# Gate rows, waiting outputs and the fill of a sorted buffer in a two-layer mixture of experts

## The chip, the cores and the metric

The kernel runs on one core of a Trainium2 chip, in float32. The metric is the device time in microseconds of one execution; the time shown is the median of several runs. A profile is one more execution, taken by the hardware profiler, with its own (longer) time.

A core has a matrix engine (TensorE, PE in the profile; PEld are its weight loads), a vector engine (VectorE, DVE), an activation engine (ScalarE, ACT), GpSimd (POOL) and SyncE (SP), which here only issues DMAs. Each engine runs its own list of instructions in order and waits on semaphores. Matrix products land in PSUM and are read from there by DVE or ACT.

## The reference, cut to what matters

Two layers work on `x` of 8 x 256 tokens of 128 numbers (16 tiles of 128 tokens). Each has a conditioning part and a mixture of 8 experts with a hidden width of 512. In the first layer every expert is computed for every token, and weighted with a gate; in the second only the two best experts of a token are.

```python
# first layer: x + ffn0(pool(x))
logits = jnp.einsum('bld,ed->ble', x, gate_weight)
kth_val = jnp.sort(logits.reshape(-1))[expert_k - 1]
gates = logits * (logits >= kth_val)
h = gelu(jnp.einsum('bld,ehd->bleh', x, w1) + b1, approximate=True)
y = jnp.einsum('bleh,edh->blde', h, w2) + b2.T[None, None]
out = jnp.einsum('blde,ble->bld', y, gates)
...
# second layer: x + ffn1(adapt(x)), with xn = layernorm(x) * gamma + beta
w, idx = jax.lax.top_k(softmax(xn @ gate_w), 2)
w = w / jnp.sum(w, axis=-1, keepdims=True)
h = gelu(jnp.einsum('bld,edh->eblh', xn, w1) + b1, approximate=False)
output = sum over experts of cw * (h @ w2 + b2) + residual
```

What matters here: the gates of the first layer need the k-th smallest of all 16384 logits, so no gate is known before all tokens have been pooled and the threshold has been found; the experts' outputs themselves don't need it.

## The kernel before, in words

**Units.** The 16 token tiles are worked in five units (`UNITS`): three of four tiles (512 columns), two of two tiles (256 columns). In `layer`, for each unit and each expert, four matmuls `hp` (w1 times the pooled tokens, 128x512 each) go to PSUM and through ACT (GELU) to `hT`; four matmuls `yp` (w2 times `hT`) accumulate in one PSUM tile of the pool `psy`, which has two buffers. Each float32 matmul shows as two passes in the trace.

**The pump.** After every `hp` and every `yp` matmul, eight times per expert, `layer` calls `pump()`. It takes one step of the coroutine at the head of `behind`, so that the small chains are spread between the matmuls in program order: first the rest of the pooling, then `threshold()` (a search for the gate limit), then `adapt(u)` for each unit whose first layer is complete. `adapt` has the second layer's front end: residual (`x2T`, `fp`), the language adapter (`adp`, `ha`, `dp`), two layer norms, the top two experts, and for each token two scatters of its row into `xs`.

**Gates.** At its end, `threshold()` sends the gate table (`gate`, transposed to `gT`) to DRAM on POOL's queue (`gd_L<-gT_L`, L415) and puts it in the dict `gd0`. From there `accumulate(u, e, ...)` loads one row of it for one unit and expert, broadcast to all 128 partitions (`gbc`, 256 KB, on SP's queue, four buffers), and VectorE multiplies the expert's output with it and sums.

**Waiting outputs.** As long as there is no gate table, ACT copies an expert's output from PSUM to SBUF (`y_first`, L782) and a closure is appended to `waiting`. When the table is there, every second pump takes one from `waiting`. A later output goes straight from PSUM to VectorE (L753) once `waiting` is empty. `accumulate` writes the accumulator at expert 0 and adds to it for the others (L755), and at expert 7 it appends `adapt(u)` to `behind`. `adapt(0)` begins with `GATES_GAP` = 20 empty steps.

The scheduler that builds the program keeps the data dependences and a priority by program order, but may put a ready instruction of an engine ahead of one that it expects to wait; the order on each engine is fixed when the program is built.

**The sorted rows.** The second layer works on `xs`, a DRAM buffer of 8 x 2048 + 128 rows of 130 numbers (520 bytes: a token, its destination row, its weight), one region per expert. It is filled beforehand with zeros and with a destination that no output has (`NOWHERE`), by one DMA on SP's queue from a tile `empty` of one row per partition (L526); before it on SP stand the weights' loads, behind it the gate rows. Tokens are then scattered into it, and 39 tiles of 128 rows are fetched, each with its expert's weights (`fetch`, `turn`, `hidden`, `output`), and scattered to `ys` by POOL. A last step gathers `ys` and adds the residual.

Of the kernel before, what the change touches and what calls it, by code (L numbers as in the profile page):

```python
# [10 lines left out]
F32 = mybir.dt.float32  # L11
I32 = mybir.dt.int32
AF = mybir.ActivationFunctionType
# [7 lines left out]
B, S, D = 8, 256, 128  # L21
P = 128
NT = B * S // P
NG = 4
GT = NT // NG
GN = GT * P

UNITS = [(0, 0, 4), (1, 0, 4), (2, 0, 4), (3, 0, 2), (3, 2, 2)]
NU = len(UNITS)
SLOTS = {2: 17, 3: 21, 4: 39}  # L30
E, HC = 8, 4
# [7 lines left out]
ROWS = E * RCAP  # L39
RW = D + 2  # L40
# [3 lines left out]
SEARCH = 16  # L44
SEARCH_GAP = 3
CHAIN_GAP = 5
GATES_GAP = 20
LEAD = 6


# [3 lines left out]
C_B10 = C_G1 + E  # L54
C_B20 = C_B10 + E * HC
# [9 lines left out]
def tile_adaln_ffn_d2(ctx: ExitStack, tc: tile.TileContext, x, ptype, lang, cols, b1v,  # L65
                      w10, w20, w11d, w21d, lw1, lw2, lgb, out):
    nc = tc.nc
# [3 lines left out]
    const = ctx.enter_context(tc.tile_pool(name="const", bufs=1))  # L71
    first = ctx.enter_context(tc.tile_pool(name="first", bufs=E))
    keep = ctx.enter_context(tc.tile_pool(name="keep", bufs=NG))
    work = ctx.enter_context(tc.tile_pool(name="work", bufs=2))
    small = ctx.enter_context(tc.tile_pool(name="small", bufs=4))
    dram = ctx.enter_context(tc.tile_pool(name="dram", bufs=1, space=DRAM))
# [23 lines left out]
    w10s, w20s = [], []  # L100
    for e in range(E):
        t = first.tile([P, WW], F32, tag="w1", name=f"w10_{e}")
        nc.sync.dma_start(out=t[:, :HC * P], in_=w10[e])
        w10s.append(t)
        t = const.tile([P, HC, D], F32, name=f"w20_{e}")
# [49 lines left out]
    for b in range(B):  # L155
        at = nc.values_load(lgi[0:1, b:b + 1], engines=(SP,), min_val=0, max_val=NL - 1,
                            skip_runtime_bounds_check_because="a language's number")
        for lst, name, src, rows, width in (
# [3 lines left out]
            t = const.tile([rows, width], F32, name=f"{name}_{b}")  # L162
# [9 lines left out]
    xT, poolT, resid, gd0 = {}, {}, {}, {}  # L172
    done = set()

    def scratch(name):
        return work.tile([P, 2, S], F32, tag="scr", name=name, bufs=NSCR)
# [82 lines left out]
    fwd, bwd, rows = fwd[:B, :], bwd[:B, :], top[:B, :]  # L259
# [88 lines left out]
    def poolings():  # L348
# [33 lines left out]
    begun = const.tile([P, NT], F32, name="begun")  # L382
# [7 lines left out]
    kth = const.tile([P, NSLOT], F32, name="kth")  # L390
    nc.gpsimd.iota(kth, pattern=[[1, NSLOT]], base=0, channel_multiplier=0,
                   allow_small_or_imprecise_dtypes=True)
    empty = const.tile([P, RW], F32, name="empty")
    nc.gpsimd.memset(empty, 0.0)

    steps = const.tile([P, SEARCH + 1, 3], I32, name="steps")
    nc.gpsimd.memset(steps, 0)
    for k, low in enumerate((*range(29, 0, -2), 0)):
        nc.gpsimd.tensor_scalar(steps[:, k, :], kth[:, 1:4], float(1 << low), None, ALU.mult)
    nowhere = const.tile([P, 1], F32, name="nowhere")  # L400
    nc.gpsimd.memset(nowhere, float(NOWHERE))

    b2p = pss.tile([E, P], F32, tag="sm", name="b2p")
# [87 lines left out]
    def top_one(v, name):  # L491
# [13 lines left out]

    xs = dram.tile([ROWS + P, RW], F32, name="xs")
    ys = dram.tile([2 * NT * P, D], F32, name="ys")
    last, lists, scatters = [None], {}, []  # L510
    used = const.tile([P, E], F32, name="used")
# [3 lines left out]
    w21 = const.tile([P, E, HC * D], F32, name="w21")  # L515


    nc.gpsimd.tensor_copy(empty.bitcast(I32)[:, D:D + 1], nowhere)
    nc.sync.dma_start(out=w11x[:, :, :HC * P], in_=w11d)
    nc.sync.dma_start(  # L520
        out=w11x[:, :, HC * P:HC * P + HC].rearrange("e p c -> p e c"),
        in_=col[:, C_B11:C_B11 + E * HC].rearrange("p (e c) -> p e c", e=E))
    nc.sync.dma_start(out=w11x[:, :, HC * P + HC:], in_=b2r.unsqueeze(1).to_broadcast([E, P, D]))
    for e in range(E):
        nc.sync.dma_start(out=w21[:, e, :], in_=w21d[e].rearrange("p c d -> p (c d)"))
    nc.sync.dma_start(out=xs.rearrange("(m p) c -> p m c", p=P),  # L526
                      in_=empty.unsqueeze(1).to_broadcast([P, (ROWS + P) // P, RW]))

    def cumulated(f, name):
        c3 = small.tile([P, E, E], F32, tag="c3", name=f"c3_{name}", bufs=2)  # L530
# [5 lines left out]
    def tiles_of(counts, edges, name):  # L536

        c2 = small.tile([P, E, NT], F32, tag="c2", name=f"c2_{name}", bufs=2)
        nc.vector.tensor_tensor(c2, counts.unsqueeze(2).to_broadcast([P, E, NT]),
                                edges.unsqueeze(1).to_broadcast([P, E, NT]), ALU.is_ge)  # L540
        f = small.tile([P, E], F32, tag="f", name=f"nf_{name}")
        nc.vector.tensor_reduce(f, c2, AX.X, ALU.add)
        return f
# [32 lines left out]
    def adapt(u, acc):  # L576
        g, o, nt = UNITS[u]
        n, t0 = nt * P, g * GT + o
        batches = range(t0 // 2, (t0 + nt) // 2)
        for _ in range(GATES_GAP if u == 0 else 0):  # L580
            yield
        x2T = work.tile([P, GN], F32, tag="x2T", name=f"x2T{u}")[:, :n]
        nc.vector.tensor_tensor(x2T, acc, xT[g][:, o * P:o * P + n], ALU.add)
        yield
# [28 lines left out]
        zr = [work.tile([P, GT, RW], F32, tag="zr", name=f"zr{u}_{s}", bufs=4)[:, :nt, :] for s in range(2)]  # L613
# [67 lines left out]
        for s, oh in enumerate((oh1, oh2)):  # L681
# [5 lines left out]
            for t in range(nt):  # L687
                move = nc.gpsimd.indirect_dma_start(  # L688
                    out=xs, out_offset=bass.IndirectOffsetOnAxis(ap=pos[:, t:t + 1], axis=0),
                    in_=zr[s][:, t, :], in_offset=None)  # L690
# [8 lines left out]
        if u in SLOTS:  # L699

            k0, k1 = SLOTS.get(u - 1, 0), SLOTS[u]
            f = tiles_of(counts, begun if u == NU - 1 else full, str(u))
# [15 lines left out]
    waiting = deque()  # L718

    def run(key, steps):  # L720
        yield from steps
        done.add(key)

    pumps = itertools.count()

    def pump():
        if waiting and gd0 and next(pumps) % 2:
            waiting.popleft()()
        if behind:
            if next(behind[0], done) is done:  # L730
                behind.popleft()

    def finished(key):
        while key not in done:
            pump()

    def layer(name, act, sources, w1s, w2s, cb1, cb2, gates, before, then):


        accs = {}  # L740

        def accumulate(u, e, y, bias):
            g, o, nt = UNITS[u]
            n, t0 = nt * P, e * NT + g * GT + o
            gbc = work.tile([P, GN], F32, tag="gbc", name=f"gbc_{name}{u}_{e}", bufs=4)[:, :n]
            nc.sync.dma_start(out=gbc, in_=gates[0][t0:t0 + nt, :].rearrange("t p -> (t p)").partition_broadcast(P))  # L746
            if e == 0:
                accs[u] = work.tile([P, GN], F32, tag="acc", name=f"acc_{name}{u}", bufs=3)[:, :n]
            part = accs[u] if e == 0 else work.tile([P, GN], F32, tag="part", name=f"part_{name}{u}_{e}")[:, :n]
            if bias is None:  # L750
                nc.vector.tensor_tensor(part, y, gbc, ALU.mult)  # L751
            else:
                nc.vector.scalar_tensor_tensor(part, y, bias, gbc, ALU.add, ALU.mult)  # L753
            if e:
                nc.vector.tensor_tensor(accs[u], accs[u], part, ALU.add)  # L755
            if e == E - 1:
                behind.append(run((name, u), then(u, accs[u])))

        for u, (g, o, nt) in enumerate(UNITS):
            n = nt * P  # L760
            finished((before, g))
            for e in range(E):
                hT = work.tile([P, HC, GN], F32, tag="hT", name=f"hT_{name}{u}_{e}")[:, :, :n]
                for c in range(HC):
                    hp = psb.tile([P, GN], F32, tag="big", name=f"hp_{name}{u}_{e}_{c}")[:, :n]
                    nc.tensor.matmul(hp, lhsT=w1s[e][:, c * P:(c + 1) * P], rhs=sources[g][:, o * P:o * P + n],  # L766
                                     start=True, stop=True)
                    nc.scalar.activation(hT[:, c, :], hp, act,  # L768
                                         bias=col[:, cb1 + e * HC + c:cb1 + e * HC + c + 1])
                    if nt == GT or c % 2:  # L770
                        pump()
                yp = psy.tile([P, GN], F32, tag="y", name=f"yp_{name}{u}_{e}")[:, :n]
                for c in range(HC):
                    nc.tensor.matmul(yp, lhsT=w2s[e][:, c, :], rhs=hT[:, c, :], start=(c == 0), stop=(c == HC - 1))  # L774
                    if nt == GT or c % 2:
                        pump()
                b2 = col[:, cb2 + e:cb2 + e + 1]
                if gates and not waiting:
                    accumulate(u, e, yp, b2)
                else:  # L780
                    y = scratch(f"y_{name}{u}_{e}").rearrange("p a b -> p (a b)")[:, :n]
                    nc.scalar.activation(y, yp, AF.Identity, bias=b2)  # L782
                    waiting.append(lambda u=u, e=e, y=y: accumulate(u, e, y, None))

    behind.append(run("poolings", poolings()))
    behind.append(run("threshold", threshold()))
    layer("first", AF.Gelu_apprx_tanh, poolT, w10s, w20s, C_B10, C_B20, gd0, "pool", adapt)


    def listing(k):  # L790
# [132 lines left out]
```

## Time and profile before

| | us |
|---|---|
| median of 3 runs (389.3 to 390.95) | 389.63 |
| the profiled execution | 397.35 |
| its span, first to last instruction | 395.6 |
| the 28 products with fresh outputs, L753 (128x512: 0.75 each) | 17.2 |
| the 8 products with waiting outputs, L751 (0.69 each) | 5.5 |
| the 8 copies of waiting outputs, L782 (0.69 each) | 5.5 |
| the fill `xs<-empty`, first to last packet | 57 to 108 |

The profile's page gives busy times by engine, then the span in 40 slices of 9.9 us with a digit for each engine's busy share in tenths and for the clock that TensorE was granted. A table of waits has: engine, what waited, `<-` what it waited for, then total us, times, longest us. The chain of waits is followed back from the last instruction and has start, us, what. The timeline has start, us, engine, line, operation, names, shapes, and in brackets the idle time before it and what ended it. Busy time by stretch has the stretch, its length, and for PE, PEld, DVE, ACT and POOL busy us and the number of instructions, then the granted clock, the DMA share and GB/s.

The stages, from the timeline: loading, scores and pooling until about 45 us; the threshold search beside unit 0's experts until 87 us; the first layer until 293 us; the second layer's 39 tiles until 381 us; the last gather until 395.6 us.

### The profile page before, as it was taken

To read this page: it belongs to the slowest core of one execution; us is meant where nothing else is said; L and a number is where in the kernel's file an instruction comes from. 1 tells how busy PE (TensorE), PEld (TensorE's weight loads), DVE (VectorE), ACT (ScalarE), POOL (GpSimd) and SP (SyncE) were. 2 spreads that over 40 slices of the span, in tenths; PEclk is the share of its full clock that TensorE was granted. 3 is DMA by queue.
4 is the path that set the end of the run, shared out by engine and by line. 5 is a ranking of instruction groups with operands and counts; after the bars stand their busy time and mean duration, and the time that the engine had idled before them with its cause. 6 is when DMAs were issued, how large, how long until landed. Compare 5 with 4: busy or idle time off the path is not lost.

```text
span 395.6 us, 5983 instructions
## 1 busy us (share of the span) xinstructions
PE 358.8 (91%) x1657; PEld 241.8 (61%) x1657; DVE 192.4 (49%) x773; ACT 172.9 (44%) x396; POOL 100.8 (25%) x161
## 2 busy tenths in 40 slices
PE   7899999999965999999999999998999869999930
PEld 7596444444422445444544578866878869999930
DVE  6368665530066666355621356665845553333305
ACT  2046345446250232424243434424454646888830
POOL 8400000000000130712070012072215553555430
PEclk9999999999996999999999999999999997999985
DMA  6935789999997211312031001125634666888417
GB/s 186 370 73 171 149 255 190 151 226 146 148 157 171 58 34 28 86 21 53 28 81 26 16 25 40 38 66 125 189 103 140 179 180 178 225 227 233 120 40 287
DMA packets 49800, 51.63 MB, mean 131 GB/s; under 512 B 6580, under 2 KB 35518, under 8 KB 49768
## 3 DMA queue, kind: packets, MB, share of 16 engines
q1 hardware_dynamic: 45128, 44.79, 50.8%
q0 software_dynamic: 2400, 4.37, 3.3%
q10 hardware_dynamic: 2240, 2.10, 1.5%
q8 instruction: 14, 0.23, 0.3%
q14 instruction: 18, 0.15, 0.1%
HBM read 36.77 MB, written 17.02 MB: 136 GB/s over the span
## 4 chain that ended last, share of the span: by engine, by line
PE 59%; POOL 9%; DMA 9%; issue 8%; DVE 8%; SPq 3%; ACT 2%; POOLq 1%; DVEq 0%; ACTq 0%
PE yp_first L774 23%; PE hp_first L766 19%; POOL ys L843 7%; DMA gbc_first<-gd_L 4%; DMA gd_L<-gT_L 3%; PE hps L824 2%; PE yps L837 2%; PE poolp L294 1%; DMA yg<-ys 1%; PE top L272 1%; PE idle L207 1%; PE dp L600 1%; PE adp L593 1%; SPq L746 1%; PE atp L212 1%
## 5 line engine op out<-in xcount | busy, mean ns | idle before, releaser
L768 ACT ACTIVATE hT_first<-hp_first,col 128x512 f32<-128x512 f32 (+1 forms) x160 | 93.0, 602 | 119.8 <-PE hp_first L766 109.7
L774 PE MATMUL yp_first<-hT_first,w 128*128 128x512 f32 (+1 forms) x320 | 124.0, 521 | 10.4 <-DVE acc_first L753 7.5
L766 PE MATMUL hp_first<-poolT,w 128*128 128x512 f32 (+1 forms) x320 | 120.7, 512 | 0.1
L774 PEld LDWEIGHTS yp_first<-hT_first,w 128*128 128x128 f32 x320 | 59.0, 193 | 55.0 <-issue 37.5
L766 PEld LDWEIGHTS hp_first<-poolT,w 128*128 128x128 f32 x320 | 59.0, 190 | 43.1 <-issue 38.4
L827 ACT ACTIVATE hs<-hps,wt 128x128 f32<-128x128 f32 x156 | 44.5, 371 | 15.0 <-PE hps L824 10.3
L843 POOL DMA_INDIRECT ys<-yt,xt x39 | 38.5, 987 | 46.9 <-ACT yt L842 34.7
L824 PE MATMUL hps<-xc,wt 128*128 128x128 f32 x312 | 43.4, 283 | 5.5 <-issue 3.2
L688 POOL DMA_INDIRECT xs<-zr,pos x32 | 31.4, 980 | 63.6 <-DVE pos L686 28.8
L824 PEld LDWEIGHTS hps<-xc,wt 128*128 128x128 f32 x312 | 39.8, 199 | 6.5 <-issue 3.4
L837 PE MATMUL yps<-w,hs 128*128 x312 | 42.1, 279 | 0.6 <-ACT hs L827 0.6
L753 DVE SCALAR_TENSOR_TENSOR part_first<-yp_first,col,gbc_first 128x512 f32<-128x512 f32 (+1 forms) x28 | 17.2, 614 | 45.8 <-PE yp_first L774 42.7
L837 PEld LDWEIGHTS yps<-w,hs 128*128 128x128 f32 x312 | 38.8, 195 | 0.9 <-ACT hs L827 0.9
L841 DVE TENSOR_TENSOR yt<-yps,wt 128x128 f32<-128x128 f32 x39 | 11.4, 291 | 45.3 <-PE yps L837 37.3
L591 POOL MEMSET ha<- 1x512 f32 x5 | 2.6, 517 | 76.2 <-PE dp L600 76.1
L842 ACT ACTIVATE yt<-yt,xt 128x128 f32<-128x128 f32 x39 | 15.8, 405 | 13.5 <-DVE yt L841 6.5
L755 DVE TENSOR_TENSOR acc_first<-acc_first,part_first 128x512 f32<-128x512 f32 (+1 forms) x35 | 20.3, 580 | 0.6
L415 POOL DMA_DIRECT2D gd_L<-gT_L x1 | 0.7, 664 | 72.7 <-DVE gT_L L413 72.7
L782 ACT ACTIVATE y_first<-yp_first,col 128x512 f32<-128x512 f32 x8 | 5.5, 687 | 27.5 <-PE yp_first L774 27.5
L817 DVE TENSOR_SCALAR xc<-xtp,col 128x128 f32<-128x128 f32 x39 | 15.7, 403 | 1.2 <-PE kp L672 0.6
L429 DVE TENSOR_SCALAR_CACHE_REDUCE fl<-logit,tr 128x128 f32<-128x128 f32 x46 | 13.6, 344 | 0.6
L751 DVE TENSOR_TENSOR acc_first<-y_first,gbc_first 128x512 f32<-128x512 f32 x1 | 0.7, 693 | 23.0 <-DMA gbc_first<-gd_L 23.0
(207 smaller groups left out, 317.5 us busy)
## 6 DMA issues: line engine op xcount, KB each, us to landing
wt<-w11x SPq DMA_DIRECT2D x39, 322.0 KB
xs<-empty SPq DMA_DIRECT2D x1, 8385.0 KB
w<-in_w_dram SPq DMA_DIRECT2D x24, 256.0 KB
gbc_first<-gd_L SPq DMA_DIRECT2D x24, 256.0 KB
xt<-xs SPq DMA_DIRECT2D x39, 65.0 KB
w11x<-in_w_dram SPq DMA_DIRECT2D x1, 2048.0 KB
gbc_first<-gd_L SPq DMA_DIRECT2D x16, 128.0 KB
lgb<-in_lgb_dram SPq DMA_DIRECT2D x8, 128.0 KB
```

Source lines behind the costliest of these rows:

```text
L688: move = nc.gpsimd.indirect_dma_start(out=xs, out_offset=bass.IndirectOffsetOnAxis(ap=pos[:, t:t + 1], axis=0), in_=zr[s][:, t, :], in_off ...
L753: nc.vector.scalar_tensor_tensor(part, y, bias, gbc, ALU.add, ALU.mult)
L755: nc.vector.tensor_tensor(accs[u], accs[u], part, ALU.add)
L766: nc.tensor.matmul(hp, lhsT=w1s[e][:, c * P:(c + 1) * P], rhs=sources[g][:, o * P:o * P + n], start=True, stop=True)
L768: nc.scalar.activation(hT[:, c, :], hp, act, bias=col[:, cb1 + e * HC + c:cb1 + e * HC + c + 1])
L774: nc.tensor.matmul(yp, lhsT=w2s[e][:, c, :], rhs=hT[:, c, :], start=(c == 0), stop=(c == HC - 1))
L817: nc.vector.tensor_scalar(xc, tp, col[:, C_LG:C_LG + 1], col[:, C_LB:C_LB + 1], ALU.mult, ALU.add)
L824: nc.tensor.matmul(hp[:, c, :], lhsT=wt[:, c * P:(c + 1) * P], rhs=xc, start=True, stop=True)
L827: nc.scalar.activation(hT[:, c, :], hp[:, c, :], AF.Gelu, bias=wt[:, HC * P + c:HC * P + c + 1])
L837: nc.tensor.matmul(yp, lhsT=hT[:, c, :], rhs=w21[:, bass.ds(ek, 1), c * D:(c + 1) * D], start=(c == 0), stop=(c == HC - 1))
L842: nc.scalar.activation(yt, yt, AF.Copy, scale=xt[:, D + 1:D + 2])
L843: move = nc.gpsimd.indirect_dma_start(out=ys, out_offset=bass.IndirectOffsetOnAxis(ap=xt.bitcast(I32)[:, D:D + 1], axis=0), in_=yt, in_off ...
```

## The change

Four things are changed:

- The fill of `xs` is written in pieces of four rows: `empty` has four rows per partition (and takes one of the four buffers of the tag `zr`), `xs` is 512 rows longer than the regions instead of 128, and each partition fills a contiguous stretch of it, in 4224 pieces of 2080 bytes instead of 16512 of 520.
- `pump` counts from the moment the gate table is in `gd0`. After `GATES_GAP` = 16 pumps it hands the table to `layer` (by the new list `gates0`) and begins with the waiting outputs: one at every fourth pump (`DRAIN`), two per expert. `adapt(0)` has no empty steps at its head any more.
- From that moment on every new output goes straight from PSUM to VectorE, also while others are waiting.
- `accumulate` takes a unit's experts in any order: the first to come begins the accumulator, a counter `missing` tells the last.

```diff
-GATES_GAP = 20
+GATES_GAP = 16
+DRAIN = 4
...
-    empty = const.tile([P, RW], F32, name="empty")
+    empty = work.tile([P, GT, RW], F32, tag="zr", name="empty", bufs=4)
...
-    nowhere = const.tile([P, 1], F32, name="nowhere")
+    nowhere = const.tile([P, GT], F32, name="nowhere")
...
-    xs = dram.tile([ROWS + P, RW], F32, name="xs")
+    xs = dram.tile([ROWS + GT * P, RW], F32, name="xs")
...
-    nc.gpsimd.tensor_copy(empty.bitcast(I32)[:, D:D + 1], nowhere)
+    nc.gpsimd.tensor_copy(empty.bitcast(I32)[:, :, D], nowhere)
...
-    nc.sync.dma_start(out=xs.rearrange("(m p) c -> p m c", p=P),
-                      in_=empty.unsqueeze(1).to_broadcast([P, (ROWS + P) // P, RW]))
+    rows = xs.rearrange("(p m t) c -> p m (t c)", p=P, t=GT)
+    nc.sync.dma_start(out=rows, in_=empty.rearrange("p t c -> p (t c)").unsqueeze(1).to_broadcast(list(rows.shape)))
...
-        for _ in range(GATES_GAP if u == 0 else 0):
-            yield
...
-    pumps = itertools.count()
+    ready = itertools.count(-GATES_GAP)
+    gates0 = []
 
     def pump():
-        if waiting and gd0 and next(pumps) % 2:
-            waiting.popleft()()
+        if gd0:
+            n = next(ready)
+            if not n:
+                gates0.append(gd0[0])
+            if waiting and n >= 0 and n % DRAIN == 0:
+                waiting.popleft()()
...
-        accs = {}
+        accs, missing = {}, [E] * NU
...
-            if e == 0:
+            begun = u in accs
+            if not begun:
                 accs[u] = work.tile([P, GN], F32, tag="acc", name=f"acc_{name}{u}", bufs=3)[:, :n]
-            part = accs[u] if e == 0 else work.tile([P, GN], F32, tag="part", name=f"part_{name}{u}_{e}")[:, :n]
+            part = work.tile([P, GN], F32, tag="part", name=f"part_{name}{u}_{e}")[:, :n] if begun else accs[u]
...
-            if e:
+            if begun:
                 nc.vector.tensor_tensor(accs[u], accs[u], part, ALU.add)
-            if e == E - 1:
+            missing[u] -= 1
+            if not missing[u]:
                 behind.append(run((name, u), then(u, accs[u])))
...
-                if gates and not waiting:
+                if gates:
                     accumulate(u, e, yp, b2)
...
-    layer("first", AF.Gelu_apprx_tanh, poolT, w10s, w20s, C_B10, C_B20, gd0, "pool", adapt)
+    layer("first", AF.Gelu_apprx_tanh, poolT, w10s, w20s, C_B10, C_B20, gates0, "pool", adapt)
```

## The prediction

> **What bounds the kernel now.** I read the page first (busy shares and slices), then the table of waits, then the chain of waits and the timeline from 80 to 130 us, then busy time by stretch, and last the packets of the DMA queues.
>
> ```profile
> span 395.6 us, 5983 instructions
> PE 358.8 (91%) x1657; PEld 241.8 (61%) x1657; DVE 192.4 (49%) x773; ACT 172.9 (44%) x396; POOL 100.8 (25%) x161
> PE   7899999999965999999999999998999869999930
> PEclk9999999999996999999999999999999997999985
> DMA  6935789999997211312031001125634666888417
> ```
>
> TensorE is the bound: a slice is 9.9 us, and PE stands at 8 or 9 from slice 1 to the tail, but for slices 11 and 12 (109 to 128 us) and slice 32 (317 to 326). In slice 12 the clock digit falls to 6. DMA is full in slices 6 to 11. That is one place, and the table of waits names it:
>
> ```profile
> DVE acc_first L751 <- DMA gbc_first<-gd_L: 23.0, 1, 23.0
> PEld yp_first L774 <- DVE acc_first L753: 8.3, 1, 8.3
> PE yp_first L774 <- DVE acc_first L753: 7.5, 1, 7.5
> ```
>
> VectorE stood 23.0 us for the first gate row; PE then stood 7.5 us for VectorE to read an output out of PSUM. The chain of waits shows how the row came late, and the timeline the end of the stall:
>
> ```profile
> 87.83 11.58 DMA gd_L<-gT_L
> 99.42 2.84 SPq L746
> 103.54 11.18 DMA gbc_first<-gd_L
> 115.56 5.32 DMA gbc_first<-gd_L
> ```
> ```profile
> 110.57 0.69 DVE L751 TENSOR_TENSOR acc_first<-y_first,gbc_first 128x512 f32<-128x512 f32 x1 [23.04 <-DMA gbc_first<-gd_L]
> 121.00 0.69 DVE L751 TENSOR_TENSOR part_first<-y_first,gbc_first 128x512 f32<-128x512 f32 x1 [0.42 <-DMA gbc_first<-gd_L]
> 122.22 0.74 DVE L753 SCALAR_TENSOR_TENSOR acc_first<-yp_first,col,gbc_first 128x512 f32<-128x512 f32 x1
> 123.02 5.84 PE L774 MATMUL yp_first<-hT_first,w 128*128 128x512 f32 x8 [7.49 <-DVE acc_first L753]
> ```
> ```profile
> 116.00:123.00 7.00, 0.00 (x0) 0.00 (x0) 6.01 (x11) 0.25 (x1) 0.00 (x0) 0.82 0.91 192
> 123.00:128.00 5.00, 4.99 (x7) 2.21 (x8) 2.42 (x4) 0.00 (x0) 0.00 (x0) 0.56 0.75 134
> ```
>
> The gate table leaves at 87.8 us and lands 11.6 us later; the first row (a 256 KB broadcast load) needs another 11. Only then do the eight waiting outputs of unit 0 go through VectorE, one after the other, from 110.6 to 122.2, and behind them stands the one instruction that PE needs: the multiply that frees the PSUM buffer of unit 1, expert 0 (L753 at 122.2). There are two such buffers, so PE stops at expert 2. Its first eight passes afterwards take 5.84 us where eight take 3.43 elsewhere in the chain: 2.4 us lost to a clock of 0.56. So this place costs 7.5 + 2.4 = 9.9 us.
>
> What fills the DMA is `xs<-empty`, 8385 KB in 520-byte packets. They run from 57 to 108 us by the packet records, on the same queue that the gate rows use; their rate changes between some 272 GB/s (57 to 62 us, 80 to 83) and some 150 (63 to 77, 88 to 107).
>
> **What the Trainium skill says.** "DMA: Bandwidth & Descriptors", section "Queues, rings and completion order": each engine consumes a queue's descriptors in ring order and goes round between queues packet by packet. The trace agrees: the gate rows, on the fill's queue, start moving in earnest only as its last packets go (packets of 2048 B from 103 us), while the table, on POOL's queue, gets through in between, late. Same page, "Why small descriptors are slow (HBM only)": a fixed 3 cycles per packet beside 32-byte beats; an estimate from it is 20 cycles for 520 B and 68 for 2080, so 15% fewer per byte. "TensorE: Matmul & The Clock Gate", part 1: the clock halves after an idle window of about 3.4 us; the trace's 7.5 us of idle with 0.56 behind it agrees. "Runtime: NRT & Kernel Launch", on the launch: a profile's total exceeds the reported time by some 6.2 us whatever the kernel.
>
> **The change part by part.** The order of instructions on each engine shows that it moves things only between 87 us and the end of unit 2; from there on it is the same to the last instruction.
>
> *1. Order of the sums.* VectorE now gets, after the first waiting output, the multiply of unit 1 expert 0, then waiting outputs and fresh ones mixed: 12 gate rows (8 of unit 0, 4 of unit 1) ahead of unit 0's final sum, where there were 8. The same 8 outputs are held back and copied by ACT. Cost in instructions: none. Effect: the multiply that frees PSUM is second in the queue instead of after eight outputs. With the loads as late as now, it would run at 111.3 to 112 us (the second row was there at 111.2) instead of 122.2. PE wants the buffer at 115.5 in the order of before, and at 118.8 in the new one, since the scheduler puts expert 4's four `hp` matmuls (eight passes, 3.43 us) ahead too. The 9.9 us go.
>
> *2. The fill.* 4224 packets of 2080 B for 16512 of 520, 2% more bytes. Nothing in the trace shows 2080-byte stores of this kind; nearest are the 2048-byte packets before it, at 300 to 375 GB/s. Bounds: no faster than now in its slow stretches (150 GB/s, end at 109), or 350 throughout (end at 82). I take 15% off: an end near 100, gate rows a few us earlier. Below nothing: 2% more bytes, 1 us. It issues nothing more on SP; POOL's memset grows from 130 to 520 columns, under 1 us before 20 us, while the fill is issued at 53.5.
>
> *3. The pause.* GATES_GAP moves from unit 0's adaptation to the pumps behind the gates: 16 pumps are two experts, so the first row is summed at the end of unit 1 expert 0. Unit 0's adaptation now begins one expert later in PE's order; its chain to the scatters keeps its spacing (16 layer matmuls from `dp` to `znp`, 4 from `l1p` to `kp`). Later units start at the same places, so nothing behind is late.
>
> *4. What is late next.* With PE unbroken from 88 us, expert 2's outputs run at 118.8 to 122.2, 3's to 125.7, 4's to 129.1, then bare on PE stand `fp`, `adp`, `dp` of unit 0. `fp` wants unit 0's sum. Its last row's load reuses the buffer that expert 2's multiply frees at 123.1; a load in the quiet stretch took 1.0 us from the freed buffer to its first packet and 2.0 to the last (130.6 to 132.7), so it lands at about 126.5. Behind it: product, two sums and x2T at 0.61 us each, done at 129.4. `fp` (0.6) is unhindered, `adp` (1.0) ends at 130.7, and `dp` waits for two 0.47 us `ha` behind `x2`: PE idle some 0.7 us. With the old row spacing (one in about 1.75 us from 110.5) the twelfth is there at 129.8 and PE loses 2.7 us instead. I take 1.0.
>
> Sum: 9.9 - 1.0 = 8.9 us off, 395.6 to 386.7 in span. The profiled execution took 397.35, of which 1.75 lie around the span; the median of the runs is 389.63, 7.7 below. The skill's 6.2 us would explain most of that as overhead, so I carry the 8.9 over whole: 380.7, and write 381.0. Everything behind it is PE-bound or hangs on PE's order (the second layer with its 39 tiles, the wait near 322 us, the tail from 381), and moves along.
>
> **The rivals.**
>
> *A, the forecast (0.80):* the stall goes, 381.0. Its own range is 378.8 (no new wait, and the 0.4 and 0.3 us that PE idles at 147 and 156 gone too) to 386.
>
> *B (0.11): the stall is mostly the profile's.* The DMA shows two speeds; had the fill run at 272 GB/s all along, it would have ended at 57.5 + 31.6 = 89 us, the table would land at about 91.5, a row at 94.5, fifteen operations of 0.61 later PSUM is free at 104, and PE never stops. Unprofiled runs, 7.7 us shorter, could look like that. Then the change brings nothing and adds its 1.0: 390.6. Against it: PE runs at full clock in the profile, and other waits must share the 7.7. A half-size stall gives some 385, within A.
>
> *C (0.09), slower: PE runs into `fp` behind the twelfth row.* In PE's fixed order nothing is left to do beside `fp`, `adp`, `dp`, where before `adp` and `dp` stood among expert 3's passes. Every microsecond that the row lands after 126.5 is one of PE's, and from some 3 us on the clock halves, 2.4 more. Loads beside other traffic took 5.3 and 11.2 us in the chain; at 5.3 the row is there at 128.5 and PE loses 2 + 1. Slower it gets only where before had little stall (B's case) and this one 3 us: 389.6 + 3 = 392.6. It decides where the loss here exceeds what before's stall cost. Against it: the fill is over by then, and single loads in quiet stretches took 3 us.
>
> That the fill isn't faster (part 2 does nothing) is no rival to the sign: 395.6 - 9.9 + 2.7, or 382.4 in time.
>
> **How the numbers follow.** A has 0.80, B 0.11, C 0.09. What this kernel's measurement can tell is about 0.5%, 2 us. A is faster, B the same, C slower. The range goes from A's best end, 378.8, to 388.0, which takes in a stall of a fifth of its profiled size, and leaves out B, C and a little of A, about 2 in 10.
>
> **What would show it.** In the profile after: no PE wait of over 2 us between 88 and 140 us and no clock below 1.0 there; the multiply of unit 1 expert 0 as VectorE's second instruction after the gates, waiting for PE or for a row but not for unit 0's sums; first-layer passes ending near 284 instead of 292; the gap from 316 to 329 moved by the same 9 us, not wider. The fill's last packet before 108 us would bear out part 2. Wrong would be: a PE wait at `fp` or `dp` of several us; a wait near 308 to 320 that grows by what was saved; or a median within 2 us of before with the profile's stall gone.

## The result, and the profile after

In the first comparison the changed kernel took 392.01 us (median of 20 runs, 389.85 to 393.8) against 389.65 us before (20 runs, 388.89 to 392.05): ratio 1.005, 95% interval 1.0031 to 1.0068. It is slower by a bare 0.5%, where 381.0 had been predicted. Four later comparisons gave 0.9887 to 0.9909; they come below, since without them this result would be misread. Ratios and intervals leave out five runs that lie more than 1.5% above the fastest of their kernel; medians and ranges take in all runs.

The profiled execution took 392.52 us, close to its median, with a span of 390.8. Its page, with the same lines as before and the GB/s of each slice:

```profile
span 390.8 us, 5982 instructions
PE 358.1 (92%) x1657; PEld 241.8 (62%) x1657; DVE 191.6 (49%) x773; ACT 171.9 (44%) x396; POOL 101.0 (26%) x161
...
PE   6899999999999999999999999979998959999920
...
PEclk9889999999999999999999999999999987999985
DMA  7936689925131500111111011127525756888227
GB/s 219 345 76 175 144 242 385 382 103 142 52 110 42 119 26 29 64 45 55 47 48 25 15 29 41 43 62 195 163 59 154 216 161 176 237 224 240 85 80 247
```

The hole in slices 11 and 12 is gone: PE stands at 9 from slice 2 to slice 25, and the clock is full from slice 3 to slice 31. The fill now runs in slices 6 and 7 at 385 and 382 GB/s and is over. What stands out is slice 32 (313 to 322 us), where PE is at 5: there was a hole there before too. The table of waits of PE (us in total, times, longest) says what is left:

```profile
PE hps L830 <- DVE xc L823: 6.8, 3, 4.5
PE yp_first L780 <- ACT hT_first L774: 3.4, 5, 1.3
...
PE dp L599 <- issue: 0.6, 1, 0.6
PE kp L670 <- DVE sofar L664: 0.5, 2, 0.3
```

The 7.5 us wait for L753 has no successor. The timeline of the first layer shows the first gate row 16 us earlier than before, and the small new waits:

```profile
94.24 0.69 DVE L756 TENSOR_TENSOR acc_first<-y_first,gbc_first 128x512 f32<-128x512 f32 x1 [5.68 <-DMA gbc_first<-gd_L]
...
130.13 0.60 PE L465 MATMUL fp<-ident,acc_first 128*128 128x128 f32 x4
130.66 1.05 PE L592 MATMUL adp<-x2T,lw 128*32 128x256 f32 x4
132.32 0.68 PE L599 MATMUL dp<-lw,ha 33*128 33x128 f32 x4 [0.61 <-issue]
...
145.57 0.62 ACT L621 COPY zr<-zr 128x512 f32<-128x512 f32 x1 [2.22 <-DVE zr L484]
146.83 1.12 PE L780 MATMUL yp_first<-hT_first,w 128*128 128x512 f32 x2 [0.78 <-ACT hT_first L774]
```

`fp` and `adp` run through; `dp` costs PE 0.61 us. At 145.57 a copy of unit 0's rows stands on ACT ahead of two GELUs and waits 2.22 us for VectorE, so the matmuls that need those GELUs lose 0.78 us. PE had had 7.5 + 2.4 us to win here; yet the span is only 4.8 us below the profiled one before, and the runs are not shorter at all. The timelines show what these 4.8 us are made of: from the copy of the gate table (`gT`) to the end of the last pass of the first layer it is 205.13 us before and 197.75 after, 7.4 less; but the table comes 1.0 us later after the change, and the second layer and the last gather take 0.8 us more each.

Of the signs that the prediction named, these came: no PE wait of over 2 us and full clock between 88 and 140 us, and the end of the fill before 108. The first layer's passes end at 286.0 us, though, not near 284, and PE's wait near 320 us ends 5 us earlier, not 9. A sign of being wrong came too: the stall of the profile is gone, and the median is no shorter than before.

### The profile page after: what moved, and what is told of

Read it like the earlier page. It is cut to its first block, busy times and chain, and to the rows that moved or that the text cites. A ratio compares the mean times of both kernels' runs of the same rounds, so it can differ in the third digit from the quotient of the medians.

```text
span 390.8 us, 5982 instructions
## 1 busy us (share of the span) xinstructions
PE 358.1 (92%) x1657; PEld 241.8 (62%) x1657; DVE 191.6 (49%) x773; ACT 171.9 (44%) x396; POOL 101.0 (26%) x161
## 4 chain that ended last, share of the span: by engine, by line
PE 61%; DVE 10%; POOL 10%; issue 9%; DMA 3%; ACT 2%; another core or an unknown queue 1%; POOLq 1%; SPq 0%; DVEq 0%; ACTq 0%
PE yp_first L780 24%; PE hp_first L772 22%; POOL ys L849 7%; PE hps L830 2%; PE yps L843 2%; DMA yg<-ys 2%; PE top L273 2%; PE poolp L295 1%; PE lgp L244 1%; PE adp L592 1%; POOL resid L620 1%; ACT hT_first L774 1%; POOL rstd_f L481 1%; PE dp L599 1%
## 5 line engine op out<-in xcount | busy, mean ns | idle before, releaser
L774 ACT ACTIVATE hT_first<-hp_first,col 128x512 f32<-128x512 f32 (+1 forms) x160 | 92.0, 602 | 109.7 <-PE hp_first L772 87.9
L780 PE MATMUL yp_first<-hT_first,w 128*128 128x512 f32 (+1 forms) x320 | 121.2, 513 | 3.5 <-ACT hT_first L774 3.4
L285 ACT ACTIVATE probs<-probs,sl 128x256 f32<-128x256 f32 x16 | 6.9, 497 | 10.9 <-DVE probs L282 10.9
```

The costliest lines, as they stand in the source:

```text
L774: nc.scalar.activation(hT[:, c, :], hp, act, bias=col[:, cb1 + e * HC + c:cb1 + e * HC + c + 1])
```

## The experiments

Three theories stood at the beginning. Theory 1: ordinary runs don't have the wait for the gates (from the third comparison on: it is large only in some), and the new order costs about 2 us. Theory 2: the wait is always there, and what is saved is given back later. Theory 3: the larger pieces cost the time. The kernels of one later comparison ran on one chip, beside runs of the kernel before, which are its base; the chip was another one each time. For the first comparison, and for the profile that the prediction was made from, no chip is on record.

### The change taken apart (second comparison)

Both kernels again, and each half of the change alone. The fill alone keeps only the hunks of the fill (cut here; the whole is in the section on the change); the order alone is everything else.

```diff
-    empty = const.tile([P, RW], F32, name="empty")
+    empty = work.tile([P, GT, RW], F32, tag="zr", name="empty", bufs=4)
...
-    xs = dram.tile([ROWS + P, RW], F32, name="xs")
+    xs = dram.tile([ROWS + GT * P, RW], F32, name="xs")
...
+    rows = xs.rearrange("(p m t) c -> p m (t c)", p=P, t=GT)
```

The kernel before, unchanged:

> The kernel before, unchanged, profiled once more and timed beside itself. Theory 1 (the stall is not in ordinary executions): its profile shows about 389 to 391 us, PE waits less than 2 us between 88 and 130 us, the fill's packets end well before 100 us. Theory 2 (the stall is always there, and what the change saves is given back later): the profile again has a PE wait of 6 to 8 us near 116 us with a clock near 0.56 behind it. Ratio 1.000 in both.

The fill alone:

> The kernel before with the fill in pieces of four rows alone. Theory 1: within 0.3% of before (389 to 390.5 us), no stall in its profile, the fill over near 80 us. Theory 2: 381 to 384 us, since the gate rows come early. Theory 3 (it is the larger pieces that cost the 2 us): 391 to 392.5 us.

The order alone:

> The pause, the mixed sums and the two per expert alone, with the old fill of 520-byte rows. Theory 1: the new order costs what the whole change costs, 391.5 to 392.5 us, with PE waits at dp and at unit 1's outputs. Theory 2: 382 to 385 us. Theory 3: within 0.3% of before.

The changed kernel, unchanged:

> The changed kernel, unchanged, on the same chip as the three others. All theories: 391.5 to 392.5 us, ratio near 1.005; it is there to be compared with them, span, clock and waits.

| second comparison | median us (range) | ratio to before, 95% interval |
|---|---|---|
| kernel before, base | 386.27 (382.58 to 389.17) | |
| kernel before, again | 386.00 (382.96 to 389.07) | 1.0002 (0.9973 to 1.0030) |
| fill alone | 380.34 (379.95 to 381.80) | 0.9875 (0.9821 to 0.9930) |
| order alone | 381.49 (380.51 to 382.81) | 0.9892 (0.9838 to 0.9946) |
| changed kernel | 382.02 (380.45 to 383.30) | 0.9908 (0.9879 to 0.9937) |

Theory 3 falls: the larger pieces alone are worth 5.9 us. Theory 1 falls as it stood: the fill alone was to gain nothing and the order alone to lose 2 us. The kernel before waits 3.6 us for the gates in its new profile, neither under 2, as theory 1 has it, nor 6 to 8, as theory 2 does. All theories had expected 391.5 to 392.5 us of the changed kernel, which took 382.02. Theory 2's times for the two halves (381 to 384 and 382 to 385) are closest. Each half alone brings the whole gain, and the fill alone more than both together. The order alone removes the wait with the old, late fill, as the timeline and the busy time of PE by stretch show (stretch, length, PE busy us, and so on):

```profile
106.23 0.69 DVE L756 TENSOR_TENSOR acc_first<-y_first,gbc_first 128x512 f32<-128x512 f32 x1 [17.21 <-DMA gbc_first<-gd_L]
106.88 0.75 DVE L758 SCALAR_TENSOR_TENSOR acc_first<-yp_first,col,gbc_first 128x512 f32<-128x512 f32 x1
```
```profile
104.00:123.00 19.00, 19.00 (x46) 8.48 (x45) 7.92 (x12) 8.24 (x12) 0.00 (x0) 1.00 0.58 142
```

The first row is as late as ever (106.2 us), but the product that frees PSUM is VectorE's next instruction, and PE is busy for 19.00 of 19.00 us. The fill alone, in the same stretch, has the first row at 94.35 us and PE busy throughout:

```profile
104.00:123.00 19.00, 19.00 (x50) 8.40 (x49) 9.26 (x16) 7.59 (x12) 0.00 (x0) 1.00 0.44 107
```

So the two halves remove the same wait, and together they remove it once.

### What the new order costs (third comparison)

The changed kernel takes 1.7 us more than the fill alone, although both lack the wait. All three were run again, on another chip, beside a kernel with the empty steps back at the head of the first unit's adapter:

```diff
         batches = range(t0 // 2, (t0 + nt) // 2)
+        for _ in range(20 if u == 0 else 0):
+            yield
```

> The changed kernel once more, to be compared with the parts beside it on whatever chip this is. On the first chip it took 392.0 against 389.65 us (ratio 1.005), on the second 382.0 against 386.3 (0.991). Theory 1 (the wait for the gate rows is large only in some executions; what the change surely costs is 1.3 to 2 us of new waits): the ratio depends on how often the kernel before shows the wait on this chip: 0.99 where its runs spread over 3 us or more with lowered clocks, 1.003 to 1.007 where they lie close together. Theory 2 (the changed kernel gets a new late stall of some 7 us near 316 us, where the output sums of the second layer wait): its profile shows the vector engine's add of L847 idle for 4 us or more, and the ratio is 1.00 or above. Theory 3 (the larger fill pieces cost the time): it is no faster than the order alone.

> The fill alone (rows filled four to a piece; the order of the sums as before). On the second chip 380.3 us, ratio 0.9875. Theory 1: no longer than the changed kernel, shorter by 1 to 2 us, on any chip, and never slower than the kernel before. Theory 2: no late stall near 316 us, ratio 0.98 to 0.99 on any chip. Theory 3: slower than the kernel before where the wait for the gates is small, by 1 to 2 us.

> The order alone (pause, mixed sums and two per expert, with the old fill). On the second chip 381.5 us, ratio 0.9892. Theory 1: within 1 us of the changed kernel on any chip, since both have the same new waits and neither the wait for the gates. Theory 2: shows the late stall near 316 us if the changed kernel does. Theory 3: shorter than the changed kernel by 2 us.

> The changed kernel with the twenty empty steps put back ahead of the first unit's adapter, so that its transposes and adapter products no longer follow at once on the last sum. Theory 1 (the new order costs time because the adapter's chain of unit 0 now runs while the vector engine still works off the double sums): the waits before dp (0.61 us), yp (0.78 us) and kp (0.26 us) go, and it takes 1.0 to 1.5 us less than the changed kernel. If the cost lies elsewhere: the same time as the changed kernel within 0.5 us, or more, since the second layer's lists come later.

| third comparison | median us (range) | ratio to before, 95% interval |
|---|---|---|
| kernel before, base | 386.43 (382.99 to 387.32) | |
| changed kernel | 381.64 (380.58 to 383.28) | 0.9887 (0.9854 to 0.9921) |
| fill alone | 379.78 (378.90 to 380.74) | 0.9831 (0.9797 to 0.9865) |
| order alone | 381.77 (381.57 to 382.68) | 0.9889 (0.9854 to 0.9925) |
| changed, with 20 empty steps | 378.66 (377.71 to 380.05) | 0.9808 (0.9775 to 0.9841) |

The empty steps bring 3.0 us, where 1.0 to 1.5 had been expected, and make the shortest kernel of all by its median (its range and that of the fill alone overlap). Where PE loses them shows in its busy time by stretch, first in the changed kernel, then in the one with the empty steps:

```profile
123.00:190.00 67.00, 64.96 (x192) 30.44 (x191) 42.48 (x148) 21.89 (x36) 17.09 (x21) 1.00 0.20 56
```
```profile
123.00:190.00 67.00, 67.00 (x188) 31.07 (x187) 37.93 (x116) 23.84 (x37) 14.80 (x17) 1.00 0.21 58
```

Without them PE idles 2.04 us of these 67: the waits before `dp` (0.61), `yp` (0.77), `kp` (0.25 and 0.26) and one of 0.14. With them, none. The adapter of unit 0 no longer meets the double sums on VectorE. The fill alone idles 0.64 us there, before `yp` (0.38) and `kp` (0.26), and so does the kernel before behind its stall; of the 2.04 us, the new order adds 1.4.

The whole cost shows in the stretch from the copy of the gate table to the end of the first layer's last pass, which differs little between profiles of one kernel without the stall. It is 193.6 us in both profiles of the fill alone, 195.6 in three of the changed kernel (second to fourth comparison), 195.5 and 195.6 in the order alone, and 192.3 with the twenty steps; in five profiles of the kernel before, with the stall in it, it is 197.0 to 201.6. So the new order costs 2.0 us there, and the steps bring 3.3; what goes beyond the idle time, 0.6 and 1.3 us, lies where the profile counts PE as busy, and is not placed.

### The late wait

In the first profiles of both kernels, and in none of the eight from the second and third comparison, PE stands near 320 us for 3 us or more. The timeline of the changed kernel in the first comparison:

```profile
314.53 0.96 POOL L687 DMA_INDIRECT xs<-zr,pos  x1 [0.40 <-issue]
315.80 0.96 POOL L687 DMA_INDIRECT xs<-zr,pos  x1 [0.30 <-issue]
317.06 0.95 POOL L687 DMA_INDIRECT xs<-zr,pos  x1 [0.30 <-issue]
318.32 0.96 POOL L687 DMA_INDIRECT xs<-zr,pos  x1 [0.30 <-issue]
319.75 0.29 DVE L847 TENSOR_TENSOR yt<-yps,wt 128x128 f32<-128x128 f32 x1 [4.67 <-remote]
320.91 0.58 PE L830 MATMUL hps<-xc,wt 128*128 128x128 f32 x1 [4.48 <-DVE xc L823]
```

VectorE's add waits 4.67 us beside four scatters, PE then waits 4.48 for VectorE, and half speed follows from 320 to 327 us. Two more comparisons asked whether this belongs to the changed kernel, to the execution or to the chip. The edit of the second kernel puts an empty step behind every single scatter of the two small units (inside the loop over a unit's tiles):

```diff
                         tc.declare_no_dep(move.ins, group=f"loads {v}", reason="full tiles get no more rows")
+                if nt < GT:
+                    yield
             yield
```

> The changed kernel once more. Open is why it was 0.5% slower than the kernel before in the first comparison and 1% faster in the two later ones. The first profiles of both kernels have one wait that none of the later ones has: the add of L847 (L841 before) idle for 4 to 5 us near 315 to 325 us, while the gather engine issues the four scatters of unit 3 in a row, with steps of the sync engine of 0.70 us in it that else take 0.03. Theory A (it belongs to the chip of the first comparison): absent here unless this is such a chip, and then the kernel before is within 1% of this one. Theory B (it comes at random in any execution): half-speed clock in some of the runs here, mean clock 0.967 or less, and those longer by 5 us or more.

> The changed kernel with an empty step of the background work between the scatters of the two small units, so that no four of them stand in a row on the gather engine. If four in a row make the late wait: on a chip that shows it in the changed kernel, the wait of 4 us falls below 1 us and the time falls by 5 to 8 us. If it has another cause, or this chip doesn't show it: the same time within 1 us, or up to 3 us more, since the lists of the last units come up to two tiles later.

In this fourth comparison the changed kernel took 381.65 (380.29 to 383.53) against 385.88 (382.12 to 389.74) before, ratio 0.9909 (0.9882 to 0.9935); with the step 381.96, ratio 0.9923 (0.9897 to 0.9949). No profile had the late wait. And the edit didn't part the four scatters; of its four in a row, the first and the last:

```profile
311.94 0.96 POOL L687 DMA_INDIRECT xs<-zr,pos  x1 [0.50 <-issue]
...
315.73 0.96 POOL L687 DMA_INDIRECT xs<-zr,pos  x1 [0.30 <-issue]
```

So the edit says nothing of the late wait. The changed kernel beside it has the same row (310.66 to 314.46 us, one each 1.27 us) without the wait: the row alone doesn't make it. (The scatters are those of the last unit, not of unit 3 as the expectation has it.)

> The changed kernel once more, for another chip. Theory A (the late wait near 316 us and the slow steps of the sync engine belong to the chip of the first comparison): ratio to the kernel before 0.987 to 0.993 again and no late wait, unless this is a chip of that kind; there the time is 388 to 394 us, the late wait stands in the profile, and the ratio is 1.00 to 1.01.

> The changed kernel with eight instead of twenty empty steps ahead of the first unit's adapter. Theory 1 (the adapter of unit 0 only has to clear the last double sums, about 4 us): eight steps are enough, and it takes 2 to 3 us less than the changed kernel, as with twenty. If the whole chain down to the copy of the rows must clear later experts' work too: only part of it, 1 us or less.

In this fifth comparison it was a chip of the other kind. The changed kernel took 391.28 us (388.12 to 392.94) and the kernel before 395.22 (391.85 to 397.47): ratio 0.9897 (0.9863 to 0.9931). The late wait is back:

```profile
321.47 0.29 DVE L847 TENSOR_TENSOR yt<-yps,wt 128x128 f32<-128x128 f32 x1 [5.38 <-remote]
...
322.13 1.22 PE L830 MATMUL hps<-xc,wt 128*128 128x128 f32 x4 [4.68 <-DVE xc L823]
```

Theory A holds for the time and the wait: all 29 runs of the two kernels on this chip are longer than any of the same kernel in comparisons two to four, by 9 to 10 us in the median. It fails for the ratio, where it had 1.00 to 1.01: the change is worth as much as elsewhere. The wait is in the first profile of the kernel before as well:

```profile
325.20 0.29 DVE L841 TENSOR_TENSOR yt<-yps,wt 128x128 f32<-128x128 f32 x1 [3.91 <-remote]
```

So theory 2 falls: it isn't what the change gives back. Eight empty steps took 390.68 us (388.31 to 391.06, 4 runs), ratio 0.9874 (0.9803 to 0.9946); 0.6 us below the changed kernel, too little to tell with so few runs. In its profile `dp` no longer waits, but `yp` and `kp` still do (0.22, 0.25, 0.35, 0.26, 0.13 us).

### How large the wait for the gates is (four single executions)

The kernel before spreads over 4.3 to 7.6 us on one chip, the changed one over 2.7 to 4.8. Four executions of the kernel before, unchanged, each with its profile, on one more chip:

> The kernel before, unchanged, one execution with its profile, the first of four. In the comparisons so far its runs spread over 5 to 7 us on one chip (382.1 to 389.7) where the changed kernel's spread over 3, and the first comparison had it at 388.9 to 392.1, next to a profile of 397.35. Theory 1 (the wait for the gate rows near 116 us differs from execution to execution, and with it the time): the wait and the half speed behind it differ between these four by more than 2 us, and the time follows them one for one within 1 us. If the spread has another source: waits alike within 1 us while the times differ by 3 us or more.

> As the first of the four; a time of 383 us or less (on a chip where the changed kernel takes 382; 390 or less where it takes 391) should go with a wait under 3 us near 116 us and no half speed behind it.

> As the first of the four; a time of 387 us or more (or 395 or more on a slow chip) should go with a wait of 5 us or more, or with half speed of 3.4 to 6.8 us behind it.

> As the first of the four. What sets the wait should be the moment at which the gate rows land: the end of the fill, near 105 us in the two profiles so far, and the landing of the gates' transposed copy behind it. If the waits differ while these moments agree within 0.5 us, something else decides.

The first gate row and the end of PE's wait in the shortest (the second) and then in the longest (the fourth):

```profile
105.47 0.69 DVE L751 TENSOR_TENSOR acc_first<-y_first,gbc_first 128x512 f32<-128x512 f32 x1 [17.90 <-DMA gbc_first<-gd_L]
...
118.67 1.55 PE L774 MATMUL yp_first<-hT_first,w 128*128 128x512 f32 x3 [3.10 <-DVE acc_first L753]
```
```profile
107.52 0.69 DVE L751 TENSOR_TENSOR acc_first<-y_first,gbc_first 128x512 f32<-128x512 f32 x1 [20.17 <-DMA gbc_first<-gd_L]
...
121.41 1.22 PE L774 MATMUL yp_first<-hT_first,w 128*128 128x512 f32 x1 [6.05 <-DVE acc_first L753]
```

And the busy time of PE from 114 to 128 us with the clock (the third number from the end), again the second, then the fourth:

```profile
114.00:128.00 14.00, 10.90 (x35) 4.88 (x34) 9.48 (x16) 1.95 (x3) 0.29 (x1) 1.00 0.67 150
```
```profile
114.00:128.00 14.00, 7.95 (x18) 3.14 (x16) 8.98 (x15) 1.74 (x3) 0.00 (x0) 0.76 0.55 163
```

All six profiles of the kernel before, by the end of the fill (its last packet):

| execution | fill ends | first row used | PE waits | half speed behind | us |
|---|---|---|---|---|---|
| second of the four | 103.4 | 105.5 | 3.10 | none | 382.92 |
| second comparison | 104.8 | 106.3 | 3.61 | none | 383.77 |
| first of the four | 105.5 | 106.7 | 4.19 | 3.4 us | 384.97 |
| third of the four | 105.7 | 107.2 | 3.91 | 3.4 us | 385.66 |
| fourth of the four | 106.4 | 107.5 | 6.05 | 6.8 us, half of it idle | 387.47 |
| the first profile | 109.1 | 110.6 | 7.49 | 6.8 us, 2.5 of it idle | 397.35 |

The later the fill ends, the later the first row, and nearly the longer the wait. A window at half speed costs 1.7 us of work (half of 3.4). Between the second and the fourth the wait differs by 2.95 us and the half speed by 1.7, together 4.65; the times by 4.55. From the copy of the gate table to the end of the first layer they differ by 4.66 us (196.95 and 201.61). Two expectations are off in a detail: the second execution was to wait less than 3 us (3.10), and of the two older profiles only one has the fill's end near 105 us (104.8; the other 109.1). Theory 1 in its later form holds: the wait is in every execution of the kernel before that was profiled, but of different size, and in these four it carries the spread. Why the fill ends at different times was not tried. The execution that the prediction was made from had the largest of the six, and the late wait on top.

## Why the prediction was wrong

**The step that failed: the 9.9 us were carried over whole.** The prediction took the wait of one execution, 7.5 + 2.4 us, and subtracted it from a median of runs that were 7.7 us shorter. Its reason was the Trainium skill's "Runtime: NRT & Kernel Launch", on the launch, which has a profile's total some 6.2 us above the reported time. The runs here show no such gap: wherever a run's span is on record, its time is 1.6 to 1.8 us above the span, profiled or not, and the changed kernel's profiled execution took 392.52 with a median of 392.01. So the 7.7 us were not overhead, and a profiled execution is not longer as such. The profiled execution, 397.35 us, has the late wait, and lies inside the range of the kernel before on the chip that has this wait too (391.85 to 397.47). The runs that the median was taken from lie below nearly all of that range. In the four single executions the wait with its half speed is 3.1, 5.9, 5.6 and 7.8 us, 5.6 in the mean; the fill alone, which removes it, gained 5.9 and 6.7 us. The term of 9.9 was mis-sized: these executions have 5.6 to give, not 9.9. Rival B saw this ("the stall is mostly the profile's") and had 0.11; it was right that the wait in ordinary runs is smaller, wrong that there is none.

**Part 1, the order: mechanism right.** "The 9.9 us go" even with the loads as late as now: the order alone has PE busy throughout with the first row at 106.2 us. The size was that of one execution.

**Part 2, the fill: wrong size, no effect on the sum.** "15% off, an end near 100" was an estimate from cycles per packet. Measured in the profile after: 57.3 to 81.6 us, 24.3 us instead of 52, so less than half the time per byte. The upper bound (350 GB/s, end at 82) was right; the lower one doesn't add up, since 8.8 MB at 150 GB/s throughout would end near 116, not 109. As the order had removed the wait already, the fill brought nothing more. Alone it would have been the better change.

**Part 3, the pause: costed at nothing; what it took away is worth 3.0 us.** "Its chain to the scatters keeps its spacing" is no argument: with the empty steps gone from the head of `adapt(0)`, the chain meets the double sums. Eight steps clear only its beginning, twenty all of it.

**Part 4, the new waits: 1.0 taken, 1.7 to 1.9 measured** in the medians against the fill alone, 2.0 in the first layer; the twenty steps that part 3 dropped remove them. `dp` waited 0.61 us (0.7 had been worked out), but the waits farther down the chain, above all the copy on ACT ahead of the GELUs, were not looked for.

With measured terms in the sum, 5.6 for the wait less 2.0 for the new order leaves 3.6 us, where 8.9 had been predicted. The four later comparisons have 3.9 to 4.8 us between their medians, and the two profiled executions of the first comparison 4.8 (397.35 and 392.52). The forecast of a faster kernel was right in these four, at about half its size.

**The first comparison stays open.** Its 1.005 follows from none of this: the corrected sum gives 386 from its base, and 392.01 was measured. Rivals B (390.6) and C (392.6) come near by luck. B wants no stall in the runs before and a new cost of 1.0 us. C wants PE to run into `fp` behind the twelfth gate row; `fp` follows without a gap. The changed kernel took nearly the same as in the comparison on a chip with the late wait (392.01 and 391.28), and the two profiles agree in PE's instructions within 0.02 us from 24 to 250 us. What differs is the kernel before: 388.9 to 392.1 us there, 391.9 to 397.5 here. Short waits hardly explain it: a wait of 3.1 us without half speed goes with 382.9 us on another chip, near the lowest time of any run of this kernel (382.1), and the lowest on the chip with the late wait is 391.85. An obvious rival is that the first comparison's runs of the kernel before came from another chip than the changed kernel's runs and the two profiles. It would account for the changed kernel's figures and for the two profiles, but times of 388.9 to 392.1 match the kernel before on none of the five later chips, and neither a chip nor a profile of these runs is on record. So the cause is not shown.

## What to carry to other kernels

A wait in one profile is a sample. Before subtracting it from a median, set the profiled execution beside the range of the runs: if it lies outside, either its largest waits are unusual, above all waits that hang on the end of a big transfer, or it doesn't come from the same chip. And two edits that remove the same wait don't add up: here the fill alone was 1.7 to 1.9 us faster than fill and order, because the second one only brought its cost. When an empty step is taken out of a chain, look at what the other engines are doing where the chain now falls, down to its last member.

## What was unexpected of the hardware

The same fill took 47.8 to 52.1 us in pieces of 520 B (16512 packets, eight profiles) and 24.3 to 24.7 in pieces of 2080 B (4224 packets, 2% more bytes, ten profiles): a packet took 54 to 59 ns in the mean at 520 B and 92 at 2080. And the end of the fill in small pieces moved by 5.6 us between executions, 103.4 to 109.1.

Four profiles, two each from the first and the fifth comparison, have a stand of VectorE and TensorE of 3 to 5 us beside four scatters near 315 to 325 us; the other fourteen have the same four scatters in a row without it. In and around that stretch (309 to 323 us) some register moves of SyncE take 0.64 to 0.71 us in these four, and none does in the others. The four also lack many of the semaphore records: 4968 to 5133 updates of semaphores against 6432 to 6470 in the others. Whether the recording makes the stand or the chip does was not tried.
